# A graph layer that fetches rows with matmuls: four units' slots at a time, h as the weights, turned back by an identity

## The chip, the core and the metric

The kernel runs on one core of a Trainium2 chip. A core has five engines that run at the same time, each in the order of its own instructions: TensorE (PE, matrix products into PSUM), VectorE (DVE), ScalarE (ACT), GpSimd (POOL, which here issues gathers) and SyncE (SP, which issues the other transfers). They wait for one another by semaphores. The metric is the time of one execution on the device in microseconds (us), the median of several runs.

## The reference

One message-passing layer of a graph network on N = 6,250 nodes with 64 features and E = 206,250 directed edges, sorted by their target:

```python
h = jnp.maximum(_layernorm(x, axis=-1), 0.0)
msg = jax.nn.relu(h[src] + edge_attr)             # E x 64
agg = jax.ops.segment_sum(msg, dst, num_segments=N)
h2 = h + agg
out = x + (jax.nn.relu(h2 @ W1 + b1) @ W2 + b2)
```

The costly part is `h[src]`: a row of 64 numbers for each of 206,250 edges, in no order. The sum over edges is easier, since edges are sorted by target.

## The kernel before

Edges are cut into groups of 768 (128 partitions x G = 6 columns). Five groups come first and are done in another way; the rest is put into 144 **units** (`GROUPS`), five units in six being two groups and the sixth one. A unit of two groups has 12 columns of edges. POOL gathers the rows of `h` for 6 of them from DRAM by an indirect transfer each (`gather`, L211). The rows for the other 2 x H = 6 columns are fetched by matmuls from a copy of `h` that lies in SBUF, `hp`: 49 parts of 128 nodes, each part a 128 x 128 tile of f16, of which 64 columns are the high and 64 the low half of a number. A unit of one group has no gathers.

The fetch by matmuls has these steps.

- **Counting** (`rank_at` ... `sourced`, L303 to L391), once for three units (a chunk): each edge gets a slot in the row of slots of its part, S = 32 slots for a part in a half unit. Out of it come, for each slot, the number of its node (`source_row` in DRAM), and for each edge, the place of its slot (`spot_rows` in DRAM). `rank_of` ends with a copy on ACT (`spot_i`, L330) that waits for DVE.
- **Loads** on SP: `source_load` and `spot_load` bring both back, repeated over all 128 partitions (384 KB each).
- **Comparisons** on DVE: `find(k)` (L538, two instructions, and two on ACT in `find_beyond`) makes `found`, a one-hot of node by slot; `back(k)` (L550, three instructions) makes `backs`, a one-hot of slot by edge.
- **`slots_of(k, bank)`** on PE (L563): for each part, 32 slots of `found` are the weights and the part of `hp` is the moving operand; four such matmuls write the four quarters of 32 partitions of one PSUM tile. That is 104 matmuls a unit, in three PSUM banks. `slots_out` (L572, ACT) copies each bank to `picked` in f16.
- **`pick(k, i)`** on PE (L578): 18 matmuls for each half unit, with `backs` as weights and `picked` moving, bring the rows to the edges.
- **`decode(k)`**: ACT scales the low half (L634), DVE adds it (L635), removes the sign trick (L637) and adds the edge attributes (L464). **`messages(k)`** (L644, ACT) is the ReLU into a tile `msg`. `one_hot` (L610) and `sums` (L658, PE) add messages up in windows of 32 targets, and `adds` (L604, DVE) adds the windows to `z`.

The order on every engine is written out by hand, in `both_units(k)`: loads for unit k+5 and k+3, `pick(k)`, `decode(k)`, `slots_of(k+1)`, the sums of unit k-1, the messages of unit k, and at the end the comparisons for unit k+2, then counting. So `find(k+2)` at the end of unit k is used by `slots_of(k+2)` in unit k+1, behind `pick(k+1)`. Gathers wait for certain matmuls of the unit before (`beats`), so that they do not run too far ahead. Edge attributes and gathered rows lie in rings of six buffers (`RING`).

## Time and profile before

| what | value |
|---|---|
| median of 3 runs | 1700.66 us (1698.28 to 1701.03) |
| the profiled execution | 1698.58 us, span 1696.9 us |
| PE, matmuls | 1129.6 us busy (67%) |
| DVE | 1042.8 us busy (61%) |
| POOL | 733.5 us busy (43%) |
| ACT | 652.8 us busy (38%) |
| granted clock of PE, mean | 0.751 |
| moved by DMA | 203.31 MB, 120 GB/s |

The span is the time from the first to the last instruction. Busy shares are averages over the whole span. A group's row in the profile gives the line, the engine, what is written and read, the count, the busy time and the mean length of one in nanoseconds, and behind the second bar the idle time of the engine just before these instructions, with what ended it. "issue" there means that no semaphore in the profile explains the idle time. The granted clock is the share of its full clock that PE was allowed; in this profile it is either 1 or 0.5 at a time.

### The profile page before, as it was taken

To read this page: it belongs to the slowest core of one execution; us is meant where nothing else is said; L and a number is where in the kernel's file an instruction comes from. 1 tells how busy PE (TensorE), PEld (TensorE's weight loads), DVE (VectorE), ACT (ScalarE), POOL (GpSimd) and SP (SyncE) were. 2 spreads that over 40 slices of the span, in tenths; PEclk is the share of its full clock that TensorE was granted. 3 is DMA by queue.
4 is the path that set the end of the run, shared out by engine and by line. 5 is a ranking of instruction groups with operands and counts; after the bars stand their busy time and mean duration, and the time that the engine had idled before them with its cause. 6 is when DMAs were issued, how large, how long until landed. Compare 5 with 4: busy or idle time off the path is not lost.

```text
span 1696.9 us, 55640 instructions
## 1 busy us (share of the span) xinstructions
PE 1129.6 (67%) x24161; PEld 950.7 (56%) x24161; DVE 1042.8 (61%) x2165; ACT 652.8 (38%) x1365; POOL 733.5 (43%) x763
## 2 busy tenths in 40 slices
PE   1367676767677767676678676666767676766775
PEld 0246555556556655555566555555655565655665
DVE  8755655656656656566466565665665655656566
ACT  3433443434334433343344343333343433334343
POOL 7644435444443344444443444544444335344330
PEclk9677777777776876777776777777677777677767
DMA  6343444434443443444443443434343444344341
GB/s 197 83 124 114 115 123 135 122 105 128 122 133 97 132 126 98 129 134 120 130 119 100 134 115 115 140 108 133 119 127 117 117 123 133 98 130 124 97 134 43
DMA packets 133652, 203.31 MB, mean 120 GB/s; under 512 B 27609, under 2 KB 101978, under 8 KB 133402
## 3 DMA queue, kind: packets, MB, share of 16 engines
q1 hardware_dynamic: 109354, 175.12, 32.9%
q0 software_dynamic: 23936, 24.56, 8.1%
q8 instruction: 190, 3.11, 0.8%
q14 instruction: 60, 0.49, 0.1%
q10 hardware_dynamic: 112, 0.03, 0.0%
HBM read 195.53 MB, written 4.09 MB: 118 GB/s over the span
## 4 chain that ended last, share of the span: by engine, by line
PE 36%; issue 18%; DVE 8%; ACT 5%; another core or an unknown queue 4%; DVEq 1%; DMA 0%; ACTq 0%
PE half L563 15%; PE pick L578 13%; PE pick L658 4%; DVE found L538 2%; DVE xg L637 1%; ACT msg L644 1%; DVE both L635 1%; DVE ea L464 1%; ACT both L634 1%; PE rows L379 1%; DVE oh L610 1%; PE rows L694 1%; ACT dist L543 1%; DVE backs L550 1%
## 5 line engine op out<-in xcount | busy, mean ns | idle before, releaser
L211 POOL DMA_INDIRECT xg<-h_rows,src_sb x730 | 711.0, 974 | 906.6 <-issue 312.2
L563 PE MATMUL half<-hp,found 128*32 128x128 f16 x14976 | 477.3, 267 | 413.9 <-issue 396.7
L563 PEld LDWEIGHTS <-found 128*32 128x32 f16 x14976 | 345.5, 119 | 531.0 <-issue 499.3
L635 DVE TENSOR_TENSOR both<-pick,both 128x384 f32<-128x384 f32 x144 | 80.0, 556 | 563.8 <-ACT both L634 554.1
L578 PE MATMUL pick<-picked,backs 128*128 128x128 f16 x5184 | 409.0, 251 | 13.5 <-issue 10.4
L578 PEld LDWEIGHTS <-backs 128*128 128x128 f16 x5184 | 385.2, 115 | 32.9 <-issue 26.0
L572 ACT CAST picked<-half 128x512 f16<-128x512 f32 x432 | 244.0, 586 | 303.2 <-remote 179.1
L550 DVE TENSOR_SCALAR backs<-spots,ids 128x1536 f16<-128x1536 int16 x432 | 280.9, 703 | 0.0
L634 ACT ACTIVATE both<-pick 128x384 f32<-128x384 f32 x144 | 70.6, 490 | 535.4 <-remote 423.4
L538 DVE TENSOR_SCALAR found<-sources,nodes_of 128x1536 f16<-128x1536 int16 x288 | 186.3, 687 | 45.5 <-issue 45.4
L658 PE MATMUL pick<-oh,msg 128*64 128x32 f32 x3224 | 175.5, 270 | 5.4 <-ACT msg L644 3.7
L658 PEld LDWEIGHTS pick<-oh,msg 128*64 128x64 f32 x3224 | 156.8, 193 | 30.6 <-issue 21.4
L464 DVE SCALAR_TENSOR_TENSOR ea<-xg,ea 128x384 f32<-128x384 f32 (+1 forms) x146 | 129.4, 887 | 5.1
L644 ACT ACTIVATE msg<-ea 128x768 f32<-128x768 f32 x144 | 114.1, 792 | 25.8 <-DVE ea L464 25.1
L637 DVE SCALAR_TENSOR_TENSOR xg<-both 128x384 f32<-128x384 f32 x144 | 80.4, 558 | 5.0
L610 DVE TENSOR_TENSOR oh<-slot,slots 128x192 f32<-128x192 int16 (+1 forms) x149 | 76.3, 512 | 2.5 <-PE rows L312 2.2
L544 ACT ACTIVATE found<-dist,ones 128x256 f16<-128x256 bf16 x144 | 73.1, 508 | 10.3 <-issue 5.7
L543 ACT ACTIVATE dist<-sources,beyond 128x256 bf16<-128x256 int16 x144 | 71.4, 495 | 0.0
L379 PE MATMUL rows<-holds,marks 128*96 128x96 f16 x288 | 27.8, 238 | 63.4 <-ACT sp L367 51.3
L379 PEld LDWEIGHTS <-marks 128*96 128x96 f16 x288 | 27.4, 152 | 69.8 <-issue 63.5
L604 DVE TENSOR_TENSOR z<-z,pick 128x32 f32 x269 | 49.5, 184 | 7.1 <-PE rows L684 2.8
L388 ACT CAST source<-rows 24x64 int16<-24x64 f32 x144 | 29.2, 202 | 32.5 <-PE rows L379 28.6
(115 smaller groups left out, 483.4 us busy)
## 6 DMA issues: line engine op xcount, KB each, us to landing
sources<-source_row SPq DMA_DIRECT2D x144, 384.0 KB
spots<-spot_rows SPq DMA_DIRECT2D x144, 384.0 KB
ea<-in_edge_attr_dram SPq DMA_DIRECT2D x115, 384.0 KB
xg<-h_rows,src_sb POOLq DMA_INDIRECT x730
ea<-in_edge_attr_dram SPq DMA_DIRECT2D x38, 192.0 KB
xb<-in_x_dram SPq DMA_DIRECT2D x12, 128.0 KB
out_dram<-o SPq DMA_DIRECT2D x12, 128.0 KB
h_rows<-x SPq DMA_DIRECT2D x3, 384.0 KB
```

Source lines behind the costliest of these rows:

```text
L211: it = nc.gpsimd.indirect_dma_start(out=xg[:, j, :], out_offset=None, in_=rows[:, :], in_offset=bass.IndirectOffsetOnAxis(ap=idx[:, j:j + ...
L464: nc.vector.scalar_tensor_tensor(y, xg, 1.0 / UP, ea, op0=ALU.mult, op1=ALU.add)
L538: nc.vector.tensor_scalar(found[k][:, b * PARTS:(b + 1) * PARTS].rearrange("p m i s -> p (m i s)"), sources[k], nodes_of[:, b:b + 1], None ...
L550: nc.vector.tensor_scalar(backs[k][:, q].rearrange("p w t s -> p (w t s)"), spots[k].rearrange("p w s -> p (w s)").bitcast(I16), ids[:, q: ...
L563: last = nc.tensor.matmul(ps[j * S:(j + 1) * S, u], found[k][:, m, i, :], hp[:, min(m, RR - 1)].rearrange("p t d -> p (t d)"), start=(b == ...
L572: nc.scalar.copy(picked[k][:, bank * 4:bank * 4 + 4], halves.pop((k, bank)))
L578: last = nc.tensor.matmul(ps[:, t * 2 * D:(t + 1) * 2 * D], backs[k][:, q % QW, q // QW, i * H + t, :], picked[k][:, i * Q + q], start=(q ...
L610: it = nc.vector.tensor_tensor(oh[:, :n], slot[:, g * G:g * G + n].unsqueeze(2).to_broadcast([P, n, W]), slots.unsqueeze(1).to_broadcast([ ...
L635: nc.vector.tensor_tensor(both, ps[:, :, :, 0], both, ALU.add)
L637: nc.vector.scalar_tensor_tensor(mine, both, -ONE_LESS, both, op0=ALU.mult, op1=ALU.max)
L644: nc.scalar.activation(msg[:, :n], eas[(k + RAWS) % RING][:, :n], AF.Relu)
L658: last = nc.tensor.matmul(pa[i * D:(i + 1) * D], msg[:, j, :], oh[:, j, :], start=(j < lo + 2), stop=(j >= G - 2))
```

## The change

- Slots are made for four units (two of the 144 "units", called a pair d here) at a time. `found[d]` has, for each part, 4 x 32 = 128 slots.
- In `across_of(d, q)` the roles are swapped: the part of `hp` is the weights (128 x 128) and the 128 slots of `found` are the moving operand. One PSUM bank takes the four parts of a quarter column q, each with one matmul for each of the two sets; for q = 0 one matmul over 512 columns comes first, for the last part. The result has features on partitions and slots along the row; ACT copies it to `across`.
- `turn_of(d, q)` turns it: four matmuls with `across` as weights and an identity (`ident_h`) as moving operand, and `turn_out` (ACT) copies to `picked`.
- A pair's six quarters are made three in each of the two units before, in between the pieces of `pick`. The first, `across_of(d+1, q)`, stands ahead of `pick(k, 0, 0)`.
- `find` and `back` compare for a whole pair in one instruction where there were two: `find(d+2)` and `find_beyond(d+2)` at the end of odd units, `back(d+1)` at the end of even ones. `source_load(d+2)` is issued in even units, `spot_load(d+2)` in odd ones, 768 KB each, into single buffers; `sources`, `spots`, `dist`, `holds` and `both` have one buffer instead of two, `oh` two instead of three.
- `messages` writes the ReLU over the edge attributes in place, one unit later in ACT's order (`messages(k-1)` in unit k).
- The rings of buffers have five entries instead of six; gathers are issued four units ahead, attributes three. Counting is done one unit earlier.
- The writes of `spot_rows` and `source_row` are two transfers each.

```diff
-RING, AHEAD = 6, 5
+RING, AHEAD = 5, 4
...
-    def find(k):
-        found[k] = hot.tile([P, PARTS * BB + J, 2, S], F16, name="found")
+    def find(d):
+        found[d] = hot.tile([P, PARTS * BB + J, 4, S], F16, name="found")
         for b in range(BB):
-            nc.vector.tensor_scalar(found[k][:, b * PARTS:(b + 1) * PARTS].rearrange("p m i s -> p (m i s)"),
-                                    sources[k], nodes_of[:, b:b + 1], None, op0=ALU.is_equal)
+            nc.vector.tensor_scalar(found[d][:, b * PARTS:(b + 1) * PARTS].rearrange("p m u s -> p (m u s)"),
+                                    sources[d], nodes_of[:, b:b + 1], None, op0=ALU.is_equal)
...
-    def slots_of(k, bank):
...
+    def across_of(d, q):
+        ps = next_half()
+        if q == 0:
+            nc.tensor.matmul(ps, hp[:, RR - 1].rearrange("p t d -> p (t d)"),
+                             found[d][:, BB * PARTS:].rearrange("p m u s -> p (m u s)"), start=True, stop=False)
+        for j in range(J):
+            m = q * J + j
+            for b in range(BB):
+                last = nc.tensor.matmul(ps[:, j * P:(j + 1) * P], hp[:, b * PARTS + m].rearrange("p t d -> p (t d)"),
+                                        found[d][:, b * PARTS + m].rearrange("p u s -> p (u s)"),
+                                        start=(b == 0 and q > 0), stop=(b == BB - 1 and (q > 0 or j == J - 1)))
+        beats.append(last)
+        across[d, q] = hot.tile([P, 4, J, S], F16, name="across")
+        nc.scalar.copy(across[d, q].rearrange("p u j s -> p j u s"), ps.rearrange("p (j u s) -> p j u s", j=J, u=4))
+
+    def turn_of(d, q):
+        ps, ac = next_half(), across.pop((d, q))
         for u in range(4):
...
+            last = nc.tensor.matmul(ps[:, u * P:(u + 1) * P], ac[:, u].rearrange("p j s -> p (j s)"), ident_h,
+                                    start=True, stop=True)
...
     def both_units(k):
         last = k == KS - 1
         if is_set(k + AHEAD):
-            load_set(k + AHEAD, beats[-6:])
-        if is_set(k + 3):
-            source_load(k + 3)
-            spot_load(k + 3)
-        pick(k, 0)
-        pick(k, 1)
+            fetch_set(k + AHEAD, beats[-6:])
+        if is_set(k + AHEAD - 1):
+            attr_set(k + AHEAD - 1)
+        d, odd = divmod(k, 2)
+        if d + 2 < KD:
+            (spot_load if odd else source_load)(d + 2)
+        more, q = d + 1 < KD, Q // 2 * odd
+        if more:
+            across_of(d + 1, q)
+        pick(k, 0, 0)
+        if more:
+            across_of(d + 1, q + 1)
+        pick(k, 0, 1)
+        if is_set(k - 1):
+            messages(k - 1)
+        if more:
+            turn_of(d + 1, q)
+            turn_out(d + 1, q)
+        pick(k, 0, 2)
+        if more:
+            across_of(d + 1, q + 2)
+        pick(k, 1, 0)
+        if more:
+            turn_of(d + 1, q + 1)
+            turn_out(d + 1, q + 1)
+        beats.append(pick(k, 1, 1))
+        beats.append(pick(k, 1, 2))
...
         decode(k)
-        if is_set(k + 1):
-            for bank in range(3):
-                slots_of(k + 1, bank)
-                slots_out(k + 1, bank)
+        if more:
+            turn_of(d + 1, q + 2)
+            turn_out(d + 1, q + 2)
         sums(k - 1)
-        messages(k)
...
-        if is_set(k + 2):
-            find(k + 2)
-            find_beyond(k + 2)
-            back(k + 2)
+        if odd and d + 2 < KD:
+            find(d + 2)
+            find_beyond(d + 2)
+        if not odd and more:
+            back(d + 1)
```

More of the change, by code (lines that the diff above doesn't have):

```diff
@@ L367, in rank_turned @@
         nc.scalar.copy(sp, turned)
-        nc.sync.dma_start(out=spot_rows[c].rearrange("w t s -> (w t) s"), in_=sp)
+        for w in range(2):
+            nc.sync.dma_start(out=spot_rows[w, c * CC:(c + 1) * CC, :], in_=sp[w * CC:(w + 1) * CC])
     lines = {}
@@ L571, in slots_out @@
[L571 to L580 removed]
+        spots.pop(d)
@@ L582, in norm_edges, with pick @@
+    def pick(k, i, t):
+        d, u = k // 2, k % 2 * 2 + i
+        ps = pick_banks[k % 2][:, i]
+        for q in range(Q):
+            last = nc.tensor.matmul(ps[:, t * 2 * D:(t + 1) * 2 * D], backs[d][:, q % QW, q // QW, u * H + t, :],
+                                    picked[d][:, q, u], start=(q == 0), stop=(q == Q - 1))
+        return last
     def norm_edges(xg):
@@ L922 @@
     find_beyond(0)
+    source_load(1)
     back(0)
-    for bank in range(3):
-        slots_of(0, bank)
-        slots_out(0, bank)
-        if bank < 2:
-            load(12 + bank, beats[-3:])
-    source_load(2)
-    spot_load(2)
+    spot_load(1)
+    for q in range(Q):
+        across_of(0, q)
+        if q:
+            turn_of(0, q - 1)
+            turn_out(0, q - 1)
+    turn_of(0, Q - 1)
+    turn_out(0, Q - 1)
     adds(-3)
+    counting(-1)
     find(1)
     find_beyond(1)
-    back(1)
     for k in range(KS):
```

139 lines of the change are left out of this document (67 added, 72 removed).

## The prediction

> **What bounds the kernel now.** I read the page first (busy shares, clock, chain, groups), then the timeline of TensorE (PE), of GpSimd (POOL) and of VectorE (DVE) in one stretch in the middle. The page:
>
> ```profile
> span 1696.9 us, 55640 instructions
> PE 1129.6 (67%) x24161; PEld 950.7 (56%) x24161; DVE 1042.8 (61%) x2165; ACT 652.8 (38%) x1365; POOL 733.5 (43%) x763
> PEclk9677777777776876777776777777677777677767
> PE 36%; issue 18%; DVE 8%; ACT 5%; another core or an unknown queue 4%; DVEq 1%; DMA 0%; ACTq 0%
> ...
> L211 POOL DMA_INDIRECT xg<-h_rows,src_sb x730 | 711.0, 974 | 906.6 <-issue 312.2
> L563 PE MATMUL half<-hp,found 128*32 128x128 f16 x14976 | 477.3, 267 | 413.9 <-issue 396.7
> L635 DVE TENSOR_TENSOR both<-pick,both 128x384 f32<-128x384 f32 x144 | 80.0, 556 | 563.8 <-ACT both L634 554.1
> L578 PE MATMUL pick<-picked,backs 128*128 128x128 f16 x5184 | 409.0, 251 | 13.5 <-issue 10.4
> L572 ACT CAST picked<-half 128x512 f16<-128x512 f32 x432 | 244.0, 586 | 303.2 <-remote 179.1
> L634 ACT ACTIVATE both<-pick 128x384 f32<-128x384 f32 x144 | 70.6, 490 | 535.4 <-remote 423.4
> L658 PE MATMUL pick<-oh,msg 128*64 128x32 f32 x3224 | 175.5, 270 | 5.4 <-ACT msg L644 3.7
> L644 ACT ACTIVATE msg<-ea 128x768 f32<-128x768 f32 x144 | 114.1, 792 | 25.8 <-DVE ea L464 25.1
> ```
>
> No engine is full. PE leads the chain, and the chain's second entry is "issue": time in which PE stands still and no semaphore explains it. One group holds nearly all of it: the 14,976 narrow matmuls of `slots_of` (L563) stood 413.9 us, 396.7 of them without a reason, while the full-width ones of `pick` (L578) stood 13.5. DVE loses 563.8 us waiting for `decode`'s input, which comes through ScalarE (ACT) from `pick`, and `pick` stands behind `slots_of` on PE. The period, from the first and last `slots_of`:
>
> ```profile
> L563 PE MATMUL half<-hp,found x14976: 216/278/314, 79.4 to 1678.8; 128*32 128x128 f16 x200
> ```
>
> (1678.8 - 79.4) / 143 steps = 11.18 us a unit, 22.37 a pair of units. What a standstill looks like (PE's timeline, then POOL's: start, length, engine, line, count, idle before):
>
> ```profile
> 698.21 1.18 PE L563 MATMUL half<-hp,found 128*32 128x128 f16 x49
> ...
> 700.61 0.29 PE L563 MATMUL half<-hp,found 128*32 128x128 f16 x4 [0.47 <-issue]
> ...
> 710.13 0.69 PE L563 MATMUL half<-hp,found 128*32 128x128 f16 x17 [1.10 <-issue]
> ...
> 712.18 4.02 PE L578 MATMUL pick<-picked,backs 128*128 128x128 f16 x36
> 716.13 1.86 PE L563 MATMUL half<-hp,found 128*32 128x128 f16 x104
> ...
> 720.63 2.17 PE L578 MATMUL pick<-picked,backs 128*128 128x128 f16 x36
> 722.73 1.64 PE L563 MATMUL half<-hp,found 128*32 128x128 f16 x104
> ```
> ```profile
> 700.00 0.94 POOL L211 DMA_INDIRECT xg<-h_rows,src_sb  x1 [0.30 <-issue]
> ...
> 713.46 0.94 POOL L211 DMA_INDIRECT xg<-h_rows,src_sb  x1 [0.30 <-issue]
> 726.24 0.94 POOL L211 DMA_INDIRECT xg<-h_rows,src_sb  x1 [11.84 <-PE rows L312]
> ```
>
> From 698 to 710 a few narrow matmuls come out every 0.7 us, with gathers on POOL; at 716 and 722, with POOL idle, all 104 take 1.64 to 1.86 us. The full-width `pick` at 712 ran under gathers without a hole (it is slow by the clock). So the hole belongs to the narrow form, or to its rate of instructions, beside gathers.
>
> **The change, part by part.** (1) *Narrow matmuls go.* A unit's 104 become 24.5 full-width ones, one of them 512 wide every second unit, and 12 for the turn: by columns 38 passes of 128. By L578's 13.5 us of idle in 5,184 I take the standstill as gone: 2.9 us a unit (413.9 / 144). Its bounds are nothing saved (it stays, below) and all. Price of a pass: 2.17 / 36 = 0.060 us at full clock, 4.02 / 36 = 0.112 at half. The array itself thus gets slower: 38 x 0.060 = 2.3 us against 1.64.
>
> The Trainium skill, "TensorE: Matmul & The Clock Gate", Part 3 (row/col tiling), speaks against the change here: outputs of 32 rows put in different column groups run at the same time. The 1.64 us for 104 agree with it; by that rule alone, with the standstill left as it is and PE the bound, 144 units gain 0.7 us each, 1800. It stands with the third rival.
>
> (2) *The order gets a new wait, and this decides the time.* The diff puts `across_of(d+1, q)` first in each unit, ahead of `pick(k, 0, 0)`. For an even unit k = 2d its weights' partner `found[d+1]` is what `find` compared at the end of unit k-1: no slack. Before, `find(k+2)` was used in unit k+1 behind `pick`. PE runs in order, so now all of an even unit's `pick` stands behind the comparison, `both` on ACT behind `pick`, and `decode` on DVE behind `both`. DVE has only counting to fill in. An odd unit's quarters use the same `found`, and `back` is made a unit ahead, so there DVE should not wait. A pair lasts: DVE's odd unit up to `find` + PE and ACT from `find` to `both` + DVE's even unit. DVE's parts, from two units (a small and a large one):
>
> ```profile
> 716.76 0.56 DVE L635 TENSOR_TENSOR both<-pick,both 128x384 f32<-128x384 f32 x1 [9.25 <-ACT both L634]
> ...
> 719.53 1.15 DVE L538 TENSOR_SCALAR found<-sources,nodes_of 128x1536 f16<-128x1536 int16 x2 [0.43 <-issue]
> 720.59 1.67 DVE L550 TENSOR_SCALAR backs<-spots,ids 128x1536 f16<-128x1536 int16 x3
> 722.18 0.45 DVE L305 TENSOR_TENSOR at<-part,from_b 128x432 f16<-128x432 f16 x1
> ...
> 735.74 0.41 DVE L323 TENSOR_TENSOR before<-before,at 128x432 f16<-128x432 f16 x1
> ...
> 736.82 0.18 DVE L329 SCALAR_TENSOR_TENSOR spot_i<-part,rank_of 128x18 int16<-128x18 f16 x1
> ...
> 745.42 0.56 DVE L635 TENSOR_TENSOR both<-pick,both 128x384 f32<-128x384 f32 x1 [7.50 <-ACT both L634]
> ...
> 748.78 1.37 DVE L538 TENSOR_SCALAR found<-sources,nodes_of 128x1536 f16<-128x1536 int16 x2 [0.43 <-issue]
> 750.07 2.05 DVE L550 TENSOR_SCALAR backs<-spots,ids 128x1536 f16<-128x1536 int16 x3
> 752.04 0.49 DVE L305 TENSOR_TENSOR at<-part,from_b 128x432 f16<-128x432 f16 x1
> ```
>
> `both` to `find`: 2.77 and 3.36 us; the two of `find`: 1.06 and 1.29; the three of `back`: 1.59 and 1.97. Five units in six are large, but the slow comparisons are not the rule, so I go two thirds of the way up: 3.16, 1.21, 1.84.
>
> (3) *Comparisons by four units*: half as many of double length. The fixed part: 3 of 1536 elements took 1.67 with steps of 0.53, so one lasts 0.61; one of 768 lasts 0.36:
>
> ```profile
> L460 DVE TENSOR_SCALAR sign<-sign 128x768 f16<-128x768 f16 x3 | 1.1, 358 | 0.1
> ```
>
> 0.61 - 0.36 = 0.25 for 768 more, 0.1 fixed, saved five times a pair (bounds: nothing, and 0.2 each). Odd unit to the end of `find`: 3.16 + 2 x 1.21 - 0.2 = 5.38. Even unit: 3.16 + 2 x 1.84 - 0.3 = 6.54.
>
> (4) *The new chain*: from `find`'s end PE runs the 512-wide one (4 passes), 24 of `across`, 36 of `pick` and 8 of two turns before `pick` is done: 72 passes, 4.3 us at full clock, 8.0 at half; then 0.49 for `both` and some 0.1 of handing over. ACT's own work in it, five copies of 0.586, a message of 0.792 and `both`, is 4.2 behind a first `across` of 0.7: 4.9, covered by PE unless the clock is full throughout. Which clock? A pair's 76 + 72 passes are 8.9 us at full clock, 11.5 with 5 us at half; window sums (175.5 / 72 = 2.4) make it 13.9. Of the some 21 us that come out below, 7 are left, nearly all in one hole ahead of `find`'s end. After such holes (the windows view: PE's share, count, ..., clock, DMA share, GB/s):
>
> ```profile
> 714.00:716.00 2.00, 2.00 (x21) 1.94 (x19) 0.00 (x0) 0.34 (x2) 0.40 (x1) 0.50 0.75 215
> 716.00:718.00 2.00, 2.00 (x108) 1.76 (x108) 1.17 (x3) 1.39 (x3) 0.00 (x0) 0.84 1.02 316
> ...
> 756.00:758.00 2.00, 1.19 (x73) 1.27 (x77) 0.53 (x1) 1.06 (x3) 0.00 (x0) 0.90 0.70 236
> ...
> 760.00:762.00 2.00, 2.00 (x24) 1.52 (x22) 1.54 (x5) 1.80 (x4) 1.35 (x2) 0.74 0.25 26
> ```
>
> PE is dense from 710.1 and the clock is full from 716.6 (0.84 of a window whose first part is at 0.5): 6.5 us at half. In the other case it falls at 757.6 and is back at 761.0: 3.4. I take 5, the middle. Then 45 passes are slow, 27 fast: 6.6, with `both` 7.2. The ends: 6.5 and 7.9.
>
> The same page of the Trainium skill, Part 1 (The HAM clock gate), says that one sustained busy window of about 3.4 us restores the clock; the second case agrees, the first took nearly two. By that rule the chain takes 6.5 and the sum below is 50 us lower.
>
> (5) *Counting.* Every third unit ACT's `spot_i` waits for DVE's, which comes behind `back`; in an even unit the next `across` copies then stand behind it on ACT. From 735.74 to the end of `spot_i` at 737.00: 1.26, some 0.2 on ACT, then 4.2 of copies, message and `both`: 5.7 of tail, 7.4 if PE has gone to half clock; 6.5 taken. That is one pair in three; another has `at` (0.49); (6.5 + 0.5) / 3 = 2.3 a pair.
>
> (6) *What I cost at nothing.* Twelve ACT copies instead of six a pair: ACT goes from 653 to some 860 us, still half idle; they fall in PE's and DVE's time, and if the odd unit's cover of about half a microsecond goes, up to 1 us a pair comes back. Loads of sources and spots, 768 KB at a time into single buffers: SP issues each behind the comparison that frees it, next need over 10 us later; with 384 KB of attributes at the 316 GB/s of the row above they take 3.7 us. Two more small writes a chunk on SP stand behind no late load. Messages in place and a ring of five: attributes are asked for three units ahead. Gathers: 730 x (0.94 + 0.30) = 905 us of POOL, four units ahead instead of five. Start and end: the first four units' slots are made alone, 76 passes at half clock, and the last pair has none: +3 (0 to +6).
>
> Sum: 5.38 + 7.2 + 6.54 + 2.3 = 21.42 us a pair, 0.95 less than 22.37; 72 pairs give 68, so 1698.6 (the profiled execution: span 1696.9 and 1.7 around it, 2 us under the median of 1700.66) - 68 + 3 = 1634; with the median's 2 us, 1636. The 2.9 us of standstill a unit are mostly handed to the new wait.
>
> **The rivals.** *Slower: the clock stays at half for the whole chain.* Speaking for it: the 6.5 us case, and 7 us of idle ahead of every chain; against it: the 3.4 case. The chain is 8.6, the tail 7.4: 5.38 + 8.6 + 6.54 + 2.63 = 23.15, 56 us more: 1758. It decides from some 6.8 us at half clock upward, where chain and tail have eaten the 0.95.
> *Full clock:* PE keeps warm, chain 4.9, tail 5.7: 18.9 a pair, 1452. Against it: the page's clock row, 6 or 7 tenths throughout. A partly warm chain lies between.
> *The standstill stays,* being a matter of gathers beside any matmul on `hp` and `found`: at least the even unit's 2.9 comes on the chain, 24.3 a pair, 1840 and more. Against it: `pick` under gathers at 712.
>
> **How the numbers follow.** Forecast 0.55 (its own range 1575 to 1700), half clock 0.26, full or nearly full clock 0.10, standstill 0.09. A measurement of this kernel tells 0.2% (3.4 us) from no change. Faster: nearly all of the first and all of the third, 0.62; same 0.04; slower 0.34. Range: up to the half-clock case without its end, and down a third of the way to full clock: 1535 to 1750.
>
> **What would show it.** Right: no idle by "issue" on the `across` and turn matmuls; PE idle of 5 to 8 us before each even unit ended by DVE `found`; DVE `both` waiting 5 to 8 us in even units and hardly in odd ones; half clock at the start of each even unit; ACT `spot_i` waiting for DVE. Wrong: holes without a releaser in `across`; DVE waiting in odd units as well (then ACT's copies bind); `found` or `backs` waiting for a DMA; DVE comparisons of more than 1.4 us.

## The result, and the profile after

The changed kernel takes 1866.47 us (median of 4 runs, 1862.72 to 1867.20) against 1699.47 us of the kernel before (4 runs, 1691.12 to 1701.03): 1.0989 times as long, with an interval of 1.095 to 1.1029. The forecast was 1636, its range ended at 1750, and its sign was wrong.

The page of the changed kernel (shares, clock, chain, the groups that matter; behind the second bar stands the idle time ahead of the group and what ended it), and the first matmul of each pair:

```profile
span 1864.0 us, 36370 instructions
PE 1156.7 (62%) x14441; PEld 1038.5 (56%) x14441; DVE 942.7 (51%) x1806; ACT 837.2 (45%) x1653; POOL 829.8 (45%) x763
PEclk9877787777778877767767777778877777777777
PE 45%; DVE 28%; ACT 10%; issue 8%; another core or an unknown queue 5%; DVEq 2%; DMA 1%; ACTq 0%; SPq 0%
L214 POOL DMA_INDIRECT xg<-h_rows,src_sb x730 | 807.9, 1107 | 982.3 <-PE rows L385 439.5
L604 PE MATMUL pick<-picked,backs 128*128 128x128 f16 x5184 | 538.1, 259 | 14.3 <-issue 12.5
L660 DVE TENSOR_TENSOR both<-pick,both 128x384 f32<-128x384 f32 x144 | 80.2, 557 | 823.4 <-ACT both L657 819.3
L580 PE MATMUL half<-found,hp 128*128 128x128 f16 x3456 | 398.3, 278 | 142.7 <-DVE found L548 108.2
L585 ACT CAST across<-half 128x512 f16<-128x512 f32 x432 | 249.8, 584 | 451.5 <-PE half L580 223.2
L590 PE MATMUL half<-ident_h,across 128*128 128x128 f16 x1728 | 206.2, 253 | 298.6 <-ACT across L585 273.4
L560 DVE TENSOR_SCALAR backs<-spots,ids 128x3072 f16<-128x3072 int16 x216 | 214.8, 1049 | 26.1 <-issue 26.1
L335 ACT ACTIVATE spot_i<-spot_i 128x18 int16<-128x18 int16 x48 | 10.4, 217 | 270.8 <-DVE spot_i L334 256.2
```
```profile
L575 PE MATMUL half<-found,hp x72: 376/380/674, 86.4 to 1816.6; 128*128 128x512 f16 x72
```

The holes of 413.9 us ahead of the slots' matmuls are gone from that line: L580 stands 142.7 us, 108.2 of them behind `find`, as it should. But DVE, which waited 563.8 us for `both`, now waits 823.4, the turn (L590) stands 298.6 us behind ACT's `across` copies, and these copies stand 451.5 us. In the chain of waits "issue" fell from 18% to 8%, while DVE went from 8% to 28% and PE from 36% to 45%; the clock row is 7 and 8 tenths, little else than before. A pair lasts (1816.6 - 86.4) / 71 = 24.37 us where 21.42 were forecast.

One pair in the timelines (start, length, engine, line, count, idle before): DVE and ACT first, then POOL and PE.

```profile
1017.66 0.56 DVE L660 TENSOR_TENSOR both<-pick,both 128x384 f32<-128x384 f32 x1 [7.91 <-ACT both L657]
...
1025.65 0.18 DVE L334 SCALAR_TENSOR_TENSOR spot_i<-part,rank_of 128x18 int16<-128x18 f16 x1
...
1031.17 0.56 DVE L660 TENSOR_TENSOR both<-pick,both 128x384 f32<-128x384 f32 x1 [4.42 <-ACT both L657]
...
1033.80 1.94 DVE L548 TENSOR_SCALAR found<-sources,nodes_of 128x3072 f16<-128x3072 int16 x2
...
1044.88 0.56 DVE L660 TENSOR_TENSOR both<-pick,both 128x384 f32<-128x384 f32 x1 [8.77 <-ACT both L657]
```
```profile
1025.87 0.22 ACT L335 ACTIVATE spot_i<-spot_i 128x18 int16<-128x18 int16 x1 [7.77 <-DVE spot_i L334]
...
1043.38 0.58 ACT L585 CAST across<-half 128x512 f16<-128x512 f32 x1 [3.35 <-remote]
```
```profile
1034.06 1.81 POOL L214 DMA_INDIRECT xg<-h_rows,src_sb  x1 [18.50 <-PE rows L385]
1036.17 0.94 POOL L214 DMA_INDIRECT xg<-h_rows,src_sb  x1 [0.30 <-issue]
...
1041.16 0.94 POOL L214 DMA_INDIRECT xg<-h_rows,src_sb  x1 [0.30 <-issue]
```
```profile
1026.61 0.61 PE L590 MATMUL half<-ident_h,across 128*128 128x128 f16 x4 [8.05 <-ACT across L585]
...
1037.14 1.06 PE L580 MATMUL half<-found,hp 128*128 128x128 f16 x8
...
1039.70 0.87 PE L580 MATMUL half<-found,hp 128*128 128x128 f16 x8
...
1040.97 0.83 PE L604 MATMUL pick<-picked,backs 128*128 128x128 f16 x12
1044.02 0.40 PE L590 MATMUL half<-ident_h,across 128*128 128x128 f16 x4 [2.23 <-ACT across L585]
```

Three things are to be seen. First the forecast wait: DVE stands 8.77 us from `find` (ends 1035.74) to `both` (1044.88). Second, a new lateness inside it: PE's third `across` quarter ends at 1040.57, yet ACT's copy of it starts at 1043.38, 2.8 us later, and PE's turn waits for this copy. In between runs the last of six gathers. The profile knows no releaser ("remote"). Third, in the odd unit ACT stands 7.77 us behind DVE's `spot_i`, with the `across` copies queued behind it, and PE 8.05 us behind these.

That the matmuls were done by 1040.57 is not certain from these rows, since the profile models their ends. The trace also records when PE's semaphore is updated, which is the message that ACT waits for. Matmuls that make such an update end at 1040.57, 1041.13, 1041.46 and 1041.80; the updates are recorded at 1043.31, 1043.41, 1043.49 and 1043.57. They lie 0.08 us apart at the end, where the six matmuls between two of them take 0.33 us. So the work was done and its messages were late, and ACT starts 0.08 us behind the first of them.

### The profile page after: what moved, and what is told of

It reads as the page before. It is cut to its first block, busy times and chain, and to the rows that moved or that the text cites. A ratio compares the mean times of both kernels' runs of the same rounds, so it can differ in the third digit from the quotient of the medians.

```text
span 1864.0 us, 36370 instructions
## 1 busy us (share of the span) xinstructions
PE 1156.7 (62%) x14441; PEld 1038.5 (56%) x14441; DVE 942.7 (51%) x1806; ACT 837.2 (45%) x1653; POOL 829.8 (45%) x763
## 3 DMA queue, kind: packets, MB, share of 16 engines
q0 software_dynamic: 23936, 24.56, 6.4%
## 4 chain that ended last, share of the span: by engine, by line
PE 45%; DVE 28%; ACT 10%; issue 8%; another core or an unknown queue 5%; DVEq 2%; DMA 1%; ACTq 0%; SPq 0%
PE pick L604 19%; PE half L580 14%; PE half L590 7%; DVE found L548 7%; DVE backs L560 5%; DVE both L660 3%; DVE xg L662 3%; ACT across L585 3%; DVE oh L636 3%; ACT picked L598 3%; ACT both L657 3%; PE pick L682 2%; DVEq L524 2%; DVE z L630 1%
## 5 line engine op out<-in xcount | busy, mean ns | idle before, releaser
L214 POOL DMA_INDIRECT xg<-h_rows,src_sb x730 | 807.9, 1107 | 982.3 <-PE rows L385 439.5
L604 PE MATMUL pick<-picked,backs 128*128 128x128 f16 x5184 | 538.1, 259 | 14.3 <-issue 12.5
L660 DVE TENSOR_TENSOR both<-pick,both 128x384 f32<-128x384 f32 x144 | 80.2, 557 | 823.4 <-ACT both L657 819.3
L580 PE MATMUL half<-found,hp 128*128 128x128 f16 x3456 | 398.3, 278 | 142.7 <-DVE found L548 108.2
L580 PEld LDWEIGHTS <-hp 128*128 128x128 f16 x3456 | 324.6, 129 | 262.3 <-issue 259.7
L585 ACT CAST across<-half 128x512 f16<-128x512 f32 x432 | 249.8, 584 | 451.5 <-PE half L580 223.2
L590 PE MATMUL half<-ident_h,across 128*128 128x128 f16 x1728 | 206.2, 253 | 298.6 <-ACT across L585 273.4
L590 PEld LDWEIGHTS <-across 128*128 128x128 f16 x1728 | 140.3, 116 | 323.6 <-ACT across L585 292.0
L560 DVE TENSOR_SCALAR backs<-spots,ids 128x3072 f16<-128x3072 int16 x216 | 214.8, 1049 | 26.1 <-issue 26.1
L548 DVE TENSOR_SCALAR found<-sources,nodes_of 128x3072 f16<-128x3072 int16 x144 | 142.1, 1029 | 19.8 <-issue 19.3
L682 PE MATMUL pick<-oh,ea 128*64 128x32 f32 x3224 | 141.7, 237 | 8.2 <-ACT ea L668 4.7
L682 PEld LDWEIGHTS pick<-oh,ea 128*64 128x64 f32 x3224 | 122.5, 152 | 29.0 <-issue 11.2
```

Of the source, the lines that this page charges most:

```text
L214: it = nc.gpsimd.indirect_dma_start(out=xg[:, j, :], out_offset=None, in_=rows[:, :], in_offset=bass.IndirectOffsetOnAxis(ap=idx[:, j:j + ...
L548: nc.vector.tensor_scalar(found[d][:, b * PARTS:(b + 1) * PARTS].rearrange("p m u s -> p (m u s)"), sources[d], nodes_of[:, b:b + 1], None ...
L560: nc.vector.tensor_scalar(backs[d][:, q].rearrange("p w t s -> p (w t s)"), spots[d].rearrange("p w s -> p (w s)").bitcast(I16), ids[:, q: ...
L580: last = nc.tensor.matmul(ps[:, j * P:(j + 1) * P], hp[:, b * PARTS + m].rearrange("p t d -> p (t d)"), found[d][:, b * PARTS + m].rearran ...
L585: nc.scalar.copy(across[d, q].rearrange("p u j s -> p j u s"), ps.rearrange("p (j u s) -> p j u s", j=J, u=4))
L590: last = nc.tensor.matmul(ps[:, u * P:(u + 1) * P], ac[:, u].rearrange("p j s -> p (j s)"), ident_h, start=True, stop=True)
```

## The experiments

Each run had runs of the kernel before beside it on the same chip; ratios are to these, and the changed kernel's is 1.0989. The medians of the kernel before lay between 1675.6 and 1700.9 us on the chips, so times of different chips are compared by ratio; 0.1 of it is some 169 us.

### Without gathers

`after_nogather` and `before_nogather`: in each kernel the gathers are left out from the 20th group on, nothing else.

```diff
-        if hi:
+        if hi and g < 20:
             gather(ring(xgs, g)[:, lo:], ...)
```

> The changed kernel, with the gathers left out from the 20th group on (the columns they fill keep what lay in the ring, so that the sums are of other rows). Theory H (hold): while a gather's transfer is under way PE is held, whatever the matmul; in the changed kernel it shows as ACT copies that start 1 to 3.5 us behind the end of their matmuls. Then these delays go, the wait from the comparisons to the next unit's input falls from 8.95 to some 6.8 us and the time to 1580 to 1700 us. Theory W (wait alone): the loss is the chain comparison, PE, ACT, decode, and gathers are harmless to full-width matmuls: within 2% of 1866 us, chain still near 9 us.

> The kernel before, with the same gathers left out. Both theories expect the holes in the narrow matmuls to go, since H says that PE is no longer held, and the narrow-form theory of the prediction says that the form stands only beside gathers: idle by issue at the slots from 414 to under 60 us, some 7 us a unit, 1050 to 1200 us. If the holes come from the rate of narrow matmuls alone (fetching of instructions), idle stays over 300 us and the time over 1550 us.

Measured: 1575.62 us, ratio 0.9401 (0.934 to 0.946), for the changed kernel, and 1189.31 us, 0.7096 (0.705 to 0.714), for the one before. The changed kernel's page, its windows view of one chain (length, then busy time and count of PE, of PE's weight loads, of DVE, ACT and POOL, then clock, DMA share, GB/s), and its first matmuls of a pair:

```profile
L660 DVE TENSOR_TENSOR both<-pick,both 128x384 f32<-128x384 f32 x144 | 79.9, 555 | 550.4 <-ACT both L657 550.4
L585 ACT CAST across<-half 128x512 f16<-128x512 f32 x432 | 250.9, 586 | 260.6 <-PE half L580 253.6
L335 ACT ACTIVATE spot_i<-spot_i 128x18 int16<-128x18 int16 x48 | 10.4, 217 | 286.9 <-DVE spot_i L334 286.9
```
```profile
1005.79:1011.69 5.90, 5.84 (x85) 5.74 (x85) 0.83 (x4) 3.91 (x8) 0.00 (x0) 0.75 0.47 167
```
```profile
L575 PE MATMUL half<-found,hp x72: 376/380/611, 84.9 to 1527.4; 128*128 128x512 f16 x72
```

And the windows of the changed kernel with its gathers, one chain after the other:

```profile
1009.75:1017.66 7.91, 7.19 (x98) 6.79 (x98) 0.00 (x1) 3.74 (x8) 4.59 (x5) 0.80 0.42 124
1035.74:1044.88 9.14, 6.86 (x89) 6.58 (x90) 0.37 (x2) 3.88 (x8) 4.84 (x6) 0.75 0.45 132
```

The chain of 7.9 to 9.1 us, at the same clock of 0.75 to 0.80 and under 4.6 to 4.8 us of gathers, takes 5.90 without them, and PE is busy nearly throughout. DVE's wait falls by 273 us, that of the `across` copies by 191; a pair lasts (1527.4 - 84.9) / 71 = 20.32 us. The block behind `spot_i` (286.9) has nothing to do with gathers. Theory H had expected 1580 to 1700, a little more; theory W fell. In the kernel before (page, then the groups of ACT with all their releasers):

```profile
L563 PE MATMUL half<-hp,found 128*32 128x128 f16 x14976 | 265.0, 225 | 49.3 <-DVE found L538 24.6
L635 DVE TENSOR_TENSOR both<-pick,both 128x384 f32<-128x384 f32 x144 | 79.6, 553 | 126.6 <-ACT both L634 126.6
```
```profile
L572 ACT CAST picked<-half 128x512 f16<-128x512 f32 x432 | 227.6, 590 | 56.3 <-PE half L563 36.8 <-remote 12.0
L634 ACT ACTIVATE both<-pick 128x384 f32<-128x384 f32 x144 | 70.1, 487 | 153.9 <-PE pick L578 148.5 <-remote 3.2 <-DVE z L604 1.1
```

The holes ahead of the narrow matmuls fall from 413.9 to 49.3 us, and with them goes another loss that the prediction's own fence shows and that it did not use: `both` (L634) stood 535.4 us, 423.4 of them for "remote"; without gathers it is 153.9 and 3.2. The copies of `slots_out` (L572) fall from 303.2 and 179.1 to 56.3 and 12.0. So gathers make two things late, narrow matmuls and PE's messages to ACT. I call both the **hold**. It costs the kernel before 1 - 0.7096 = 0.290 (some 490 us) and the changed one 1.0989 - 0.9401 = 0.159 (some 270 us). The change cut it nearly in half; it did not remove it.

The updates of PE's semaphore tell the same. I call one late if the last matmul that makes one had ended over 0.3 us before. From 200 us on, 428 of the 1,312 recorded in the changed kernel are late, half of them by more than 1.1 us, and 220 of 906 in the kernel before; nearly all fall while a gather runs on POOL or within 1.8 us of one. In the two runs without gathers not one is late. Of the updates of ACT and DVE none is seen late, but in the kernels with gathers some of theirs are not recorded at all.

### What in a gather holds

`after_plain_sp` and `after_plain_pool` replace each gather, from the 20th group on, by a plain transfer of the same size and pieces, issued by SP or by POOL. `after_near` keeps the indirect gathers and gives each of them the list 0 to 127.

```diff
+            for j in range(lo, hi):
+                r = (g * G + j) % 48 * P
+                it = nc.sync.dma_start(out=ring(xgs, g)[:, j, :], in_=h_rows[r:r + P, :])   # or nc.gpsimd
```
```diff
-                in_offset=bass.IndirectOffsetOnAxis(ap=idx[:, j:j + 1], axis=0))
+                in_offset=bass.IndirectOffsetOnAxis(ap=idx[:, j:j + 1] if rows is x else near, axis=0))
```

> The changed kernel, where from the 20th group on each gather is a plain transfer of 128 rows in a row of h_rows (the same 32 KB in pieces of 256 bytes, the same place, the same pace), issued by SP. Three theories of what holds PE's signals, each with the two ends seen so far (1866 us with gathers, 1576 without): the descriptors that POOL makes (G): this one falls to 1570 to 1630; the transfers themselves, whoever asks for them (T): it stays at 1800 to 1880; the reading by index (I): it falls to 1570 to 1630 as under G, but so does the one issued by POOL. The rows fetched are wrong ones, and the output with them.

> The same plain transfers, issued by POOL. G (POOL makes descriptors for these too): 1780 to 1880. T: 1800 to 1880. I (only reading by index holds): 1570 to 1630. The rows fetched are wrong ones.

> The changed kernel, still with indirect gathers at the same places and pace, but each reads the same 128 consecutive rows of h_rows (its list of indices is 0 to 127). Plain transfers of such rows issued by POOL gave 1577.7. If the hold comes of the gather as an instruction (POOL reading a list and making a descriptor for each entry): 1800 to 1880. If it comes of rows at random places in HBM: 1570 to 1640. The rows fetched are wrong ones.

Measured: 1575.26 us (0.9259, 0.923 to 0.929) by SP, 1577.7 us (0.9273, 0.924 to 0.930) by POOL, 1832.41 us (1.0903, 1.079 to 1.102) with near rows. From the pages of the second and the third, groups and one DMA queue:

```profile
L233 POOL DMA_DIRECT2D xg<-h_rows x679 | 488.7, 728 | 892.3 <-PE rows L391 437.4
L666 DVE TENSOR_TENSOR both<-pick,both 128x384 f32<-128x384 f32 x144 | 79.9, 555 | 549.1 <-ACT both L663 549.1
...
q0 software_dynamic: 23936, 24.56, 5.2%
```
```profile
L216 POOL DMA_INDIRECT xg<-h_rows,near x730 | 802.0, 1099 | 955.1 <-PE rows L387 436.8
L662 DVE TENSOR_TENSOR both<-pick,both 128x384 f32<-128x384 f32 x144 | 80.1, 556 | 794.6 <-ACT both L659 786.7
```

The plain transfers use the same engine and the same queue, with as many packets and bytes (23,936 and 24.56 MB in the changed kernel too), and DVE's wait is what it is without any. No update of PE's semaphore is late in either run with plain transfers; with near rows 436 of 1,292 are. So neither the bytes nor POOL's issuing (728 ns busy for each plain transfer, 1099 for each gather) holds PE's messages by itself. The indirect form does, even where all its rows are the same 128. What in that form does it, no run here shows, and the plain form was not tried in the kernel before, so that it spares the narrow matmuls too is not shown.

`before_unpaced` takes away, in the kernel before, the waits that space the gathers out.

```diff
-            load_set(k + AHEAD, beats[-6:])
+            load_set(k + AHEAD, ())
```

> The kernel before, whose gathers wait no longer for matmuls of the unit before: they go as soon as their buffer is free, one behind the other. If what is lost goes by the time that gathers are in flight (H): they are 0.94 us each in a row instead of 0.94 and some 0.30 between, and all six fall into one stretch, so the hold's 490 us shrink to between a half and three quarters: 1430 to 1560. If it goes by the number of gathers that meet narrow matmuls (N): 1660 to 1720.

Measured: 1763.16 us, 1.0363 (1.023 to 1.050), outside both expectations. From its page:

```profile
L211 POOL DMA_INDIRECT xg<-h_rows,src_sb x730 | 727.3, 996 | 944.8 <-DVE ea L464 741.8
L563 PE MATMUL half<-hp,found 128*32 128x128 f16 x14976 | 460.5, 256 | 443.3 <-issue 426.4
```

POOL now waits for buffers (`ea`, 741.8 us) instead of matmuls, the gathers come in one row behind `decode`, and the holes of the narrow matmuls grow from 413.9 to 443.3 us. So the place of the gathers matters, not only their number.

### Number or place

`after_twothirds` leaves out the middle one of every three gathers. `after_moved` keeps all and moves them: those issued in an even unit wait for that unit's `both`, at the end of the chain, and the odd unit's follow without a wait of their own.

```diff
+            if g >= 20 and j == 1:
+                continue
```
```diff
-        if is_set(k + AHEAD):
-            fetch_set(k + AHEAD, beats[-6:])
+        if is_set(k + AHEAD) and k % 2:
+            fetch_set(k + AHEAD, ())
...
         decode(k)
+        if is_set(k + AHEAD) and not odd:
+            fetch_set(k + AHEAD, done * 6)   # done: decode's both
```

> The changed kernel with every third gather left out from the 20th group on (some 226 of 679). If each gather costs alike (the hold goes by their count: 290 us for 679): 97 less, 1750 to 1785. If a unit loses the same once any gather is in flight in it: 1830 to 1866. If only gathers beyond what PE's idle time takes cost: 1600 to 1700. Those rows are left out of the sums.

> The changed kernel with all its gathers, moved: those issued in an even unit wait for that unit's both (the end of the chain from find), those of the odd unit follow without a wait of their own. So the chain, in which 4.9 of a pair's 11.0 us of gathers lie now, should be nearly free of them. Where gathers lie decides (P): the chain goes from 8.9 back to 6.0 to 6.8 as with two thirds of them or none, and the rest of the pair bears some more of them: 1630 to 1740. How many there are decides (C): 1830 to 1870. If they then run beyond find's end, since 15 us have to fit into some 15: 1740 to 1830.

Measured: 1626.5 us, 0.9701 (0.966 to 0.974), and 1787.7 us, 1.0541 (1.051 to 1.057). A third fewer gathers gives back 0.129 of the hold's 0.159 (1626.5 lies where the last theory put it, by which only gathers beyond PE's idle time cost); a mere move gives back 0.045, within its last expectation, that they run beyond the end of `find`. The stretches of a pair, means over 64 pairs, worked out from the starts and ends of DVE's `found` and `both` and of POOL's gathers (in us; in brackets the time in which POOL was busy with a gather, or with a plain transfer in that row):

| kernel | `find` to even `both` | even to odd `both` | odd `both` to `find` | pair |
|---|---|---|---|---|
| forecast | 7.2 | 8.84 | 5.38 | 21.42 |
| without gathers | 5.93 (0) | 9.81 (0) | 4.85 (0) | 20.59 |
| plain, by POOL | 6.09 (1.86) | 9.63 (2.47) | 4.87 (2.88) | 20.59 |
| two thirds of them | 6.33 (2.65) | 10.00 (2.34) | 4.93 (2.71) | 21.27 |
| moved | 7.38 (2.29) | 11.53 (7.35) | 4.89 (1.99) | 23.79 |
| near rows | 9.07 (5.19) | 10.41 (2.77) | 4.89 (2.96) | 24.36 |
| changed kernel | 8.94 (4.90) | 10.95 (3.20) | 4.89 (2.89) | 24.78 |

The last column but one holds 2 to 3 us of gathers and does not move: there DVE works through its own list, and what PE's messages do meanwhile costs nothing. In the chain gathers cost, up to 3 us. Within the changed kernel, too, chains with more of them are longer (correlation 0.81 over the 64); this alone shows no cause, since a longer chain has room for more gathers, and in `after_twothirds` the correlation is 0.20. In `after_moved` the gathers, up to 12 in a row, do not all end before the next chain. Here `find` ends at 1010.16 and `both` starts at 1018.17, with gathers up to 1016.23:

```profile
1008.21 1.95 DVE L548 TENSOR_SCALAR found<-sources,nodes_of 128x3072 f16<-128x3072 int16 x2 [0.43 <-issue]
...
1018.17 0.56 DVE L662 TENSOR_TENSOR both<-pick,both 128x384 f32<-128x384 f32 x1 [5.81 <-ACT both L659]
```
```profile
1015.29 0.94 POOL L214 DMA_INDIRECT xg<-h_rows,src_sb  x1 [0.30 <-issue]
1019.00 1.14 POOL L214 DMA_INDIRECT xg<-h_rows,src_sb  x1 [2.77 <-DVE both L662]
...
1021.90 1.70 POOL L214 DMA_INDIRECT xg<-h_rows,src_sb  x1 [0.30 <-issue]
```

They also lengthen the middle stretch, where ACT and PE hand over as well. So place matters beside number, as far as there is a place where no handover is awaited; for 15 us of gathers a pair there is too little of it. Their time alone is not the measure (2.65 us cost 0.4 in one kernel, 2.29 cost 1.45 in the other), and why is open.

### The order

`after_pickfirst` changes even units of the changed kernel: `pick`, the message, `decode` and the sums of the unit before come ahead of the `across` quarters. `pickfirst_unpaced` is the same kernel on another chip (its name misleads: nothing in its pace differs). `pickfirst_nogather` is that order without gathers. `before_slotsfirst` gives the kernel before the wait: `slots_of(k+1)` ahead of `pick(k)`.

```diff
+        early = more and not odd
+        if early:
+            lasts = [pick(k, i, t) for i in range(2) for t in range(H)]
+            beats.extend(lasts[-2:])
+            if is_set(k - 1):
+                messages(k - 1)
+            decode(k)
+            sums(k - 1)
         if more:
             across_of(d + 1, q)
-        pick(k, 0, 0)
+        if not early:
+            pick(k, 0, 0)
...
```

> The changed kernel with one thing undone in the order: in even units all of pick, the old messages, decode and the sums stand ahead of the three quarters that need the new comparisons. Theory W: the input of decode no longer stands behind the comparisons; DVE's wait of 8.6 us in front of even units falls under 3 us, a pair goes from 24.6 to 17.5 to 20 us, 1360 to 1540 us. If the wait is only covered by something else (ACT's copies, PE's time, the hold), the pair stays over 22.5 us, over 1720 us.

> The version of the changed kernel with pick ahead of across in even units, once more on this chip, with its gathers paced as they were: the earlier run gave 1644.5, so 1630 to 1665 by every theory; it is there so that versions built on it can be compared.

> Pick ahead of across in even units, and no gathers from the 20th group on. The changed kernel without gathers took 1575.6 and 20.4 us a pair, of which 5.9 are the chain from the end of find to both in even units. W (this wait is what is left): the chain goes, and a pair lasts what DVE works (some 13 us) or what PE needs (11.5 to 14): 14 to 16.5 us a pair, 1130 to 1310. If PE's full-width work or ACT's copies bound the kernel without gathers, wait or no wait: 1480 to 1580. Those rows are left out of the sums.

> The kernel before with the new wait alone: the slots of the next unit stand ahead of pick in each unit, so that they need the comparisons made at the end of the unit before. Theory W: each unit then holds a chain from find through slots (1.8 us and 2.9 of holes), pick (2 to 4) and both (0.6) that only back and counting cover: 12.5 to 14 us a unit, 1900 to 2110 us. If order costs nothing: 1700 us within 2%.

Measured: 1644.5 us, 0.9812 (0.975 to 0.987); 1677.69 us (one run, 0.9864 of the 1700.87 beside it); 1359.5 us, 0.8089 (0.801 to 0.817); 2355.57 us, 1.4055 (1.397 to 1.414). One order costs the changed kernel 1.0989 - 0.9812 = 0.118 with gathers and 0.9401 - 0.8089 = 0.131 without: some 200 to 220 us, whichever way. It is the forecast wait. I had expected more of both, since I took DVE for the next bound; in the one without gathers ACT's block behind `spot_i` is still there, and DVE still waits:

```profile
L660 DVE TENSOR_TENSOR both<-pick,both 128x384 f32<-128x384 f32 x144 | 80.1, 556 | 331.0 <-ACT both L657 329.7
L335 ACT ACTIVATE spot_i<-spot_i 128x18 int16<-128x18 int16 x48 | 10.4, 217 | 194.3 <-DVE spot_i L334 190.5
```

The same wait put into the kernel before costs some 680 us, where I had expected 225 to 435. There the narrow matmuls and their holes lie in the chain, but the holes are hardly more than they were (407.6 us by "issue" against 396.7), and so are ACT's waits for "remote" (635.1 us, all ahead of the slots' copies, against 179.1 there and 423.4 ahead of `both`). The mean clock, however, falls from 0.75 to 0.64, and the matmuls of the slots and of `pick` take 262 us more. That this is the excess is likely, but no run shows it.

### The block behind `spot_i`

In `after_spotlate` and `before_spotlate` ACT's `spot_i` copy is issued one unit later, ahead of the transpose that reads it. `pickfirst_spotlate` has the order with pick first as well, with the sums back behind `across`; `after_spotlate_moved` has the moved gathers.

```diff
     def rank_of(c):
...
-        nc.scalar.activation(spot_i[c][:, 1], spot_i[c][:, 0], AF.Copy, bias=-float(STEP * J * QW))
...
     def rank_turn(c):
+        nc.scalar.activation(spot_i[c][:, 1], spot_i[c][:, 0], AF.Copy, bias=-float(STEP * J * QW))
```

> The changed kernel with ACT's spot_i copy issued one unit later, ahead of the transpose that reads it, so that ACT no longer stands behind DVE's counting in the units with rank_of. The prediction's term for this block is 2.3 us a pair, of which some 2.1 are the block itself: 150 us less than the changed kernel, 1700 to 1740. If the chain through PE is as late anyway: 1820 to 1860.

> The kernel before, with only the spot_i copy one unit later. ACT stood 54.7 us there ahead of both and its copies: between nothing and 55 us less, 1640 to 1700. If the changed kernel's 140 us for the same edit came of the edit and not of the changed order, this one gains 100 and more too.

> Both orders together: pick ahead of across in even units with the sums back behind across, and the spot_i copy one unit later. With pick first alone PE stood 115 us ahead of the sums behind ACT's message, and ACT 175 behind spot_i: 60 to 150 us less than the 1678 of that kernel, 1530 to 1620. If the hold by gathers fills the time again: 1640 to 1680.

> The same, and the spot_i copy one unit later (which alone gave 1719.9, 22.7 us a pair with a chain of 9.1). P: 2.3 to 3.1 us less a pair, 1510 to 1565. C: 1700 to 1720.

Measured: 1719.9 us, 1.0234 (1.012 to 1.034); 1699.34 us, 1.0135 (1.009 to 1.018); 1579.66 us, 0.9399 (0.928 to 0.952); 1683.63 us, 0.9917 (0.990 to 0.994). The block costs the changed kernel 1.0989 - 1.0234 = 0.076, some 128 us. In the kernel before, where I had expected up to 55 us less, the edit costs 1.4%. PE's transpose (L361) now stands 96.2 us there instead of 35.5, most of it for a copy that has only just been issued:

```profile
L361 PE MATMUL rows<-ident_b,spot_i 128*36 128x128 bf16 x48 | 12.4, 258 | 96.2 <-ACT spot_i L359 66.8
```

So it is the change that makes a cost of it, by putting `across` copies behind it on ACT. Gathers moved on top give 0.032 more; 1683.63 lies outside both expectations. The page of `pickfirst_spotlate` and its first matmuls of a pair:

```profile
L585 ACT CAST across<-half 128x512 f16<-128x512 f32 x432 | 248.9, 587 | 348.0 <-PE half L580 186.1
L660 DVE TENSOR_TENSOR both<-pick,both 128x384 f32<-128x384 f32 x144 | 79.9, 555 | 542.0 <-ACT both L657 524.4
```
```profile
L575 PE MATMUL half<-found,hp x72: 379/379/634, 83.5 to 1534.2; 128*128 128x512 f16 x72
```

(1534.2 - 83.5) / 71 = 20.43 us a pair. With gathers and all, it is 6% faster than the kernel before: the mechanism was worth having once its two waits were out of the way.

### One step further

`pickfirst_all` uses this order in odd units too, with the sums ahead of the last turn; `pickfirst_all_sums` has them right behind `decode`. The lines are those of `pickfirst_all` against `pickfirst_spotlate`.

```diff
-        early = more and not odd
+        lasts = [pick(k, i, t) for i in range(2) for t in range(H)]
...
             turn_out(d + 1, q + 1)
+        sums(k - 1)
+        if more:
+            turn_of(d + 1, q + 2)
```

> Pick, decode and the message ahead of all across quarters in odd units too (so far only in even ones), the sums of the unit before ahead of the last turn, the spot_i copy late. In the version with even units alone DVE still stood some 8 us ahead of an odd unit's both, since pick's pieces stood between quarters there; comparisons then come early in every pair. If that wait was the bound: 2 to 4 us of 21.5 a pair, 1330 to 1450. If gathers hold PE's signals for the same total time (290 us) and only the place moves: 1540 to 1600.

> The same, with the sums of the unit before straight behind decode's pick instead of ahead of the last turn. PE then has 0.9 us of other work ahead of across, and none between the turns, which wait for ACT's copies: 10 to 60 us more than the version with the sums behind.

Measured: 1588.23 us, 0.945 (0.941 to 0.949), and 1636.22 us, 0.9759 (0.972 to 0.980). Nothing is gained over 0.9399, and the time lies where its second theory put it: with pick early the hold would meet other handovers. That it does, no run was made to show. The sums in between the turns, where PE otherwise waits for ACT's copies, are worth 48 us.

## Why the prediction was wrong

**The step that failed is (1), the standstill**: "By L578's 13.5 us of idle in 5,184 I take the standstill as gone." I read it as a property of the narrow form, because a full-width `pick` ran under gathers without a hole. A `pick` of 36 matmuls hands nothing over until its end; its own idle time cannot show a late message. The page showed this elsewhere: `both` behind `pick` stood 423.4 us for "remote". The rival "the standstill stays, being a matter of gathers beside any matmul on `hp` and `found`" (24.3 a pair, 1840 and more; chance 0.09) gave the result nearly to the number (24.37, 1866), though it is the handovers behind those matmuls that stand. That the number fits so well is luck: the gathers cost 24.37 - 20.32 = 4.05 us a pair where it had 2.9, and the rest takes 20.32 where it had 21.42, so that two misses of 1.1 us cancel. The runs put 0.159 of the time before, some 270 us, on this step; without gathers the changed kernel takes 0.940 of the time before, less than the 0.962 (1636 / 1700.66) forecast.

**(2) The new wait**: right in place and kind. It is worth 0.118 to 0.131, and DVE waits 8.77 us in the even unit shown. That odd units hardly wait was wrong, and the text had named this as a sign of it. Over the 64 pairs DVE waits 4.6 us in the 22 odd units behind `spot_i`, of which the one shown (4.42) is one, 7.3 in 11 others, of which more under (6), and 1.6 in the remaining 31; without gathers these are 4.8, 5.8 and 0.

**(3) Comparisons by four units**: right, and a little undervalued: one of double length takes 1049 ns (L560), where the forecast's own pieces give 2 x 0.61 - 0.1 = 1.12. The odd unit to the end of `find` came out at 4.85 to 4.89 us instead of 5.38; in the pair shown `both` to `find` is 2.63 (I took 3.16) and `find` 1.94 (I took 2.22).

**(4) The chain**: 5.93 us without gathers against 7.2 forecast. Of it 3.0 us are at half clock by the trace's record of the clock, where I took 5. With gathers it is 8.94, 4.5 of them at half clock, and the 5 was nearly right. In the chain shown, PE is dense from 1035.80, and the 8 matmuls at 1037.14 take 1.06 us, those at 1039.70 only 0.87, since the full clock starts among them: 4.4 us by the record. Over 64 chains this time is 2.5 to 5.7 us, with and without gathers; its median is 4.2 with them and 2.9 without. By the Trainium skill, "TensorE: Matmul & The Clock Gate", Part 1 (The HAM clock gate), one sustained window of about 3.4 us brings the full clock; the medians lie on both sides of it. The rival of half clock throughout fell: none of the 64 chains is so. One sum there is off without consequence: 148 passes with 5 us at half clock are 11.2 us, not 11.5.

**(5) The block**: forecast 2.3 us a pair, measured 10.95 - 8.70 = 2.25 (the middle stretch of `after_spotlate` is 8.70 by the same working). The size is right, and as forecast it is the copies behind it, those of the odd unit, that stand, as the ACT row at 1025.87 shows. Without gathers the pairs with it have a middle stretch of 13.52 us where others have 6.34, 22 of the 64, so 2.5 a pair.

**(6) What I cost at nothing**: for ACT's copies this held. Without gathers 31 of the 64 pairs have neither the block nor what follows; in them the middle stretch is 6.34 us against 6.54 for DVE's even unit alone, and DVE does not wait. Another term was not in the sum at all: in 11 of the 64 pairs the matmuls of the output layer (`rows` from `z`; L684 before, L708 now) stand on PE ahead of the odd unit's quarters and wait for DVE's `z`. There the middle stretch is 12.16 us without gathers, so (12.16 - 6.34) x 11 / 64 = 1.0 us a pair. The group in the kernel before, and the wait in the changed one (us in total, times, longest):

```profile
L684 PE MATMUL rows<-z,w_sb 128*64 128x256 f32 (+1 forms) x50 | 11.4, 531 | 1.2 <-ACT h L686 0.6 <-ACT msg L644 0.2
```
```profile
PE rows L708 <- DVE z L630: 27.2, 10, 3.3
```

That loads cost nothing held: `found` and `backs` stood 19.8 and 26.1 us in the whole run.

The balance, in parts of the time before: the hold shrank from 0.290 to 0.159, a gain of 0.131 or some 220 us; everything else grew from 0.7096 to 0.9401, a loss of 0.231 or some 390 us, of which the wait for `find` is 0.131 and the block 0.076 (measured with gathers); the output's matmuls, 1.0 us a pair or 0.04, were not tried by a run, and parts measured one at a time need not add up. The forecast had the first at 414 us and the second at some 350.

## What to carry to other kernels

An engine's idle time is a sign of lateness only where something is handed to it: before putting a stall down to one instruction form, look at how late the *next* engine starts behind it, and whether "remote" or "issue" sums of that size stand at other lines in the same stretches. Leaving the suspected transfers out of the kernel before would have told, in one run, that they cost 29% of it and are not bound to narrow matmuls. When a reordering puts fresh comparisons ahead of old work on an in-order engine, count every engine behind it: here one order cost 12 to 13%, a small copy on ACT 7.6%, and with both mended the same mechanism was 6% faster.

## What the hardware showed that I had not expected

- Indirect gathers on POOL make PE's narrow matmuls stall (413.9 us against 49.3 without) and its messages to ACT late; plain transfers through the same queue, with the same packets, leave the messages in time (0.9273 against 1.0903 with near rows). The Trainium skill, "SBUF — State Buffer", section "SBUF: two separate sides", says: "PE, ACT, and DVE's dedicated pair never wait on anyone." These runs do not contradict it, since what they show late are semaphore updates of work that is done, not reads; what holds them, and what stalls the narrow matmuls, is open.
- A gather takes 0.94 us, but 1.81 where it runs beside DVE's comparisons (at 1034.06, `found` from 1033.80), and on average 1107 ns in the changed kernel against 974 before. The box "The 'DVE blocks DMA' trap (SWDGE)" in the same section says that POOL cannot write descriptors while a DVE instruction in a two-port mode holds the ports that they share; the trace agrees in kind, though it does not show in which mode the comparisons run. In `after_moved`, which put gathers beside `backs`, single ones took 1.70.
- Taking the spacing out of the gathers cost the kernel before 3.6%, with no gather more.
